# A state-space layer with routed experts: one written order of single operations for TensorE, VectorE and ACT, and expert blocks behind the eighth round

## The chip, the core and the metric

The kernel runs on one core of a Trainium2 chip. A core has five engines with queues of their own: TensorE (PE) for matrix products, with a separate row in the profile for its weight loads (PEld); VectorE (DVE); ScalarE (ACT); GpSimd (POOL); and SyncE (SP), which issues DMAs. An engine works through its own queue in order and waits on semaphores for the others. Products land in PSUM, which this kernel uses as eight tiles (banks) of 512 float32 columns; everything else lives in SBUF. The metric is the device time of one execution in microseconds, and the figure for a kernel is the median of several executions.

## What is computed

4096 tokens of 256 features go through a Mamba-style layer, a layer norm, a mixture of eight experts of which each token takes one, and a second layer norm. Cut to what matters:

```python
xz = x @ W_in                                   # 256 -> 1024: conv half, gate half
conv = silu(causal_conv4(xz[:, :512]) + conv_b)
d = conv @ W_x                                  # 33 columns: delta, B (16), C (16)
delta = softplus(d[:, :1])
h_t = exp(delta * -exp(A_log)) * h_(t-1) + delta * B * conv[:, :16]
ssm = sum(h_t * C, over the 16 states)
y = (ssm + conv * D_param) * silu(xz[:, 512:])
x1 = layernorm(x + y @ W_out)
e = argmax(x1 @ Wr.T + br)                      # one of eight experts
out = layernorm(x1 + relu(x1 @ W1[e].T + b1[e]) @ W2[e].T + b2[e])
```

## The kernel before

The tokens are cut into eight blocks of 512 (`TB`, `NB`), and each block passes through stages in successive rounds of the loop over `k` (line 1047). In round `k` block `k` is projected, block `k-1` (called `a`) gets its state scan, block `k-2` (`b`) its gate and output projection, and block `k-3` (`c`) its place in the experts' lists. The pieces are functions:

- `project(i, c)` (line 729): chunk `c` of eight of the input projection, into one of three PSUM banks with the tag `mm`. For chunks 0 to 3 ACT then copies it to `xc` (line 761) and starts the convolution in `acc` (763); DVE adds three taps (`taps`, 720) and ACT applies Silu (772). For chunks 4 to 7 ACT applies Silu for the gate (759).
- `gauge` (780) projects to delta, B and C; `gauge_out` (794) turns the result by TensorE transposes, and a run of small DVE operations works out softplus by a series (lines 815 to 837), each on 128 x 4 numbers and mostly on the one before it. ACT gives the exponential (816).
- `scan` (841): transposes (846), the decay's exponential on ACT (848), the scan on DVE (852), and the product with C as two pieces `hC` of 256 columns (860).
- `gate` (865): two pairs of float32 products with a matrix of ones, 16 rows each (872), sum over the states; DVE adds the skip (879), and DVE or POOL multiplies with the gate (884).
- `look` and `look_out` (886, 901) work out the router's share of x; `router_behind` (484) works out W_out times the router's weights in two halves of small products, in rounds 1 and 2.
- `project_out(i, j)` (916): output projection of 128 tokens, residual, statistics; with the last of four, the layer norm's rows and their store to DRAM. `choose` (948) picks the expert, `rank` (974) and `place` (1014) enter each token in its expert's list. The row masks of line 1008 run on POOL, and on DVE for the last three blocks.
- `table` (284), called by `blocks_of` (1027), turns counts into a table of expert blocks of 128 rows; `tokens_of` (1036) looks up the rows. 17 of the 32 blocks can be known before the last tokens are placed (`EARLY`).
- `blocks` (680) runs the expert blocks in quarters: `expert(n)` (714) advances by n. Weights are fetched by POOL's indirect DMAs (522) into three slots, rows by line 504; results are scattered by line 650.

The order on TensorE is the one written here, by the `manual_schedule` of line 120. The orders on DVE, ACT and POOL come from the scheduler, which takes what it thinks is ready first. The expert quarters of the first blocks stand between the projections of rounds 6 and 7:

```python
fill = {NB - 2: (0, 0, 0, 0, 0, 0, 2, 2), NB - 1: (1, 1, 2, 1, 1, 1, 1, 1)}.get(k, (0,) * 8)
```

Behind the loop the last blocks' stages drain between further quarters, written out one by one (lines 1112 to 1156).

These banks are three with the tag `mm`, three with `o` (state sums, output projections, expert outputs) and two with `tr` (everything small or turned).

Of the kernel before, what the change touches and what calls it, by code (L numbers as in the profile page):

```python
# [37 lines left out]
F32 = mybir.dt.float32  # L38
# [9 lines left out]
P = 128  # L48
# [45 lines left out]


# [4 lines left out]
def mamba_moe(  # L100
# [142 lines left out]
    nc.gpsimd.memset(sr, 0.0)  # L243
    ones8 = const.tile([P, NE], F32, name="ones8")
# [239 lines left out]
    def router_behind(half):  # L484
        po = bank("tr", f"pwo{half}", 2)
        pov = po[:, 0 : CC * NE].rearrange("p (c e) -> p c e", e=NE)
        cs = slice(half * CC // 2, (half + 1) * CC // 2)
        for c in range(CC)[cs]:
            for dc in range(DC):
                nc.tensor.matmul(  # L490
                    pov[:, c, :], lhsT=woutT[:, dc, c * P : (c + 1) * P], rhs=wr[:, dc, 0:NE],
                    start=(dc == 0), stop=(dc == DC - 1),
                )
        nc.scalar.copy(wout[:, cs, D : D + NE], pov[:, cs, :])

# [224 lines left out]
    def taps(i, c):  # L720
        acc, xc = st[i]["acc", c], st[i]["xc"]
        for k in range(KC - 1):
            nc.vector.scalar_tensor_tensor(  # L723
                acc, xc[:, c, k : k + TB], cw[:, c, k : k + 1], acc, ALU.mult, ALU.add
            )

    banks = {}

    def project(i, c):
# [3 lines left out]
        if c == 0:  # L733
            if i == 0:
                s["xc"] = a2.tile([P, CC, KC - 1 + TB], F32, tag="xc", name="xc0")
                nc.gpsimd.memset(s["xc"][:, :, 0 : KC - 1], 0.0)
            s["cv"] = a3.tile([P, CC, TB], F32, tag="cv", name=f"cv{i}")
            s["sg"] = a3.tile([P, CC, TB], F32, tag="sg", name=f"sg{i}")
        xc, cv, sg = s["xc"], s["cv"], s["sg"]
# [17 lines left out]
        pm = banks.pop(c)  # L757
        if c >= CC:
            evicted = nc.scalar.activation(sg[:, c - CC, :], pm, AF.Silu)  # L759
        else:  # L760
            nc.scalar.copy(xc[:, c, KC - 1 :], pm)  # L761
            acc = a3.tile([P, TB], F32, tag="acc", name=f"acc{i}_{c}")
            evicted = nc.scalar.activation(  # L763
                acc, pm, AF.Identity, scale=cw[:, c, KC - 1 : KC], bias=cb[:, c : c + 1]
            )
            s["acc", c] = acc
            if c < CC - 1:
                taps(i, c)
        if ("acc", c - 2) in s:

            with tc.issue_after(evicted.ins):
                nc.scalar.activation(cv[:, c - 2, :], s["acc", c - 2], AF.Silu)
        if c == CC and i + 1 < NB:

            after = st[i + 1]["xc"] = a2.tile(
                [P, CC, KC - 1 + TB], F32, tag="xc", name=f"xc{i + 1}"
            )
            nc.gpsimd.tensor_copy(after[:, :, 0 : KC - 1], xc[:, :, TB : TB + KC - 1])

    def gauge(i):  # L780


        s_, cv = st[i], st[i]["cv"]
        px = bank("tr", f"px{i}", 2)
        for c in range(CC):
            g = c % 2 * H
            nc.tensor.matmul(
                px[g : g + H, :], lhsT=wx[:, c, :], rhs=cv[:, c, :],
                start=(c < 2), stop=(c >= CC - 2), tile_position=(0, g),
            )  # L790
        s_["pxs"] = a2.tile([P, TB], F32, tag="pxs", name=f"pxs{i}", bufs=1)
        nc.scalar.copy(s_["pxs"], px)

    def gauge_out(i):

        s_ = st[i]
        px = bank("tr", f"pxo{i}", 2)
        for j in range(JT):
            at = slice(j * P, (j + 1) * P)
            nc.tensor.transpose(px[:, at], s_["pxs"][:, at], ident)  # L800
        pxv = px.rearrange("p (j h n) -> p j h n", h=P // H, n=H)

        def by_state(a):
            return a.unsqueeze(2).to_broadcast([P, JT, NS])

        xd = a2.tile([P, JT, XW], F32, tag="xd", name=f"xd{i}", bufs=1)

        parts = a2.tile([P, JT, 2, XW], F32, tag="parts", name=f"parts{i}", bufs=1)
        nc.scalar.copy(parts, pxv[:, :, :, 0:XW])
        nc.vector.tensor_tensor(xd, parts[:, :, 0, :], parts[:, :, 1, :], ALU.add)  # L810
        nc.scalar.copy(sr[:, :, RC : RC + NS], xd[:, :, 1 + NS : XW])
        x0 = xd[:, :, 0]

        e = a2.tile([P, JT], F32, tag="e", name=f"e{i}")
        nc.vector.scalar_tensor_tensor(e, x0, -1.0, x0, ALU.mult, ALU.min)
        grown = nc.scalar.activation(e, e, AF.Exp)
        if i == 0:
            with tc.issue_after(grown.ins):
                nc.scalar.activation(nega, al, AF.Exp)
            nc.vector.tensor_scalar(nega, nega, -1.0, None, ALU.mult)  # L820
        s = a2.tile([P, JT], F32, tag="s", name=f"s{i}")
        nc.vector.tensor_scalar(s, e, 2.0, None, ALU.add)
        nc.vector.reciprocal(s, s)
        nc.vector.tensor_tensor(s, s, e, ALU.mult)
        w = a2.tile([P, JT], F32, tag="w", name=f"w{i}")
        nc.vector.tensor_tensor(w, s, s, ALU.mult)
        q = a2.tile([P, JT], F32, tag="q", name=f"q{i}")
        nc.vector.tensor_scalar(q, w, LOG_SERIES[-1], None, ALU.mult)
        for a in LOG_SERIES[-2::-1]:
            nc.vector.scalar_tensor_tensor(q, q, a, w, ALU.add, ALU.mult)  # L830
        nc.vector.scalar_tensor_tensor(q, q, 1.0, s, ALU.add, ALU.mult)
        delta = a2.tile([P, JT], F32, tag="delta", name=f"delta{i}")
        nc.vector.tensor_scalar(delta, x0, 0.0, None, ALU.max)
        nc.vector.scalar_tensor_tensor(
            sr[:, :, RD : RD + NS], by_state(q), 2.0, by_state(delta), ALU.mult, ALU.add
        )
        nc.vector.tensor_tensor(
            sr[:, :, RB : RB + NS], xd[:, :, 1 : 1 + NS], sr[:, :, RD : RD + NS], ALU.mult
        )

    def scan(i):
        s_, cv = st[i], st[i]["cv"]
        hbefore = st[i - 1]["h"] if i else None
        pt = bank("tr", f"pt{i}", 2)
        for j in range(JT):
            nc.tensor.transpose(pt[0:NR, j * P : (j + 1) * P], sr[:, j, :], ident)
        dA = a2.tile([NS, TB], F32, tag="dA", name=f"dA{i}", bufs=1)
        nc.scalar.activation(dA, pt[RD : RD + NS, :], AF.Exp, scale=nega)
        dBx = a2.tile([NS, TB], F32, tag="dBx", name=f"dBx{i}", bufs=1)
        nc.vector.tensor_tensor(dBx, pt[RB : RB + NS, :], cv[0:NS, 0, :], ALU.mult)  # L850
        h = a2.tile([NS, TB], F32, tag="h", name=f"h{i}")
        nc.vector.tensor_tensor_scan(
            h, dA, dBx, 0.0 if hbefore is None else hbefore[:, TB - 1 : TB],
# [353 lines left out]
```

## Time and profile before

| | |
|---|---|
| median of three executions | 479.17 us (476.85 to 479.68) |
| the profiled execution | 479.7 us, its span 478.0 us |
| mean granted TensorE clock | 0.993 |
| first projection product | 4.4 us |
| last projection product | 225.3 us |
| ACT table loads of line 759 (Silu) | 12, mean 1283 ns |
| DVE taps, line 723 | 96, mean 777 ns |
| POOL row masks, line 1008 | 20, mean 1307 ns |
| TensorE's waits for DVE's `sg` ahead of line 920 | 0.9 us, once |

The span runs from the first to the last instruction; the execution's own time has 1.7 us around it. A row of the profile's groups names the source line, the engine, the operation, then output and inputs by the program's names; behind the bar stand busy time and the mean of one. TensorE's matmul rows overlap, so the time that one of them holds the engine is read from the starts of neighbours in the timeline. A float32 product is recorded as two rows.

### The profile page before, as it was taken

The numbers are of one execution on the slowest core, as the hardware profiler recorded it, in microseconds if no ns is written. First come the engines' busy times: TensorE is split into PE (matmuls) and PEld (weight loads), VectorE is DVE, ScalarE is ACT, GpSimd is POOL, SyncE is SP. The second block draws the span as 40 slices with busy tenths as digits, with TensorE's granted clock in tenths as the row PEclk, the third lists the DMA queues.
The fourth block names the chain that finished last, engine by engine and source line by source line (L and its number), as shares of the span: only waits on it lengthen the run. The fifth ranks groups of instructions, "written<-read, shape, count | busy, mean of one in ns | idle before, by whom it ended". The sixth has DMA issues, their size and how long they took to land. (4 is left out here: it accounts for less than half of the span.)

```text
span 478.0 us, 7559 instructions
## 1 busy us (share of the span) xinstructions
PE 466.2 (98%) x2606; PEld 350.1 (73%) x2606; DVE 340.4 (71%) x1120; ACT 223.4 (47%) x453; POOL 185.5 (39%) x194
## 2 busy tenths in 40 slices
PE   8999999999999999999999999999999999999994
PEld 6444554645455566677788999999989898989884
DVE  1687959899898997986998978755446565645453
ACT  3776767886896877584625131212212121212111
POOL 2001203442418372450433423435445456654541
PEclk9998999999999999999999999999999999999998
DMA  8401012040124945250766759799997279977910
GB/s 237 166 1 45 0 42 91 1 132 0 47 87 149 431 159 188 110 199 18 271 242 225 270 209 366 260 368 350 359 347 277 60 253 345 313 247 245 353 44 22
DMA packets 23401, 89.98 MB, mean 188 GB/s; under 512 B 4914, under 2 KB 14909, under 8 KB 19650
## 3 DMA queue, kind: packets, MB, share of 16 engines
q0 software_dynamic: 8752, 74.71, 42.7%
q1 hardware_dynamic: 13650, 14.50, 9.3%
q8 instruction: 21, 0.34, 0.3%
q10 hardware_dynamic: 960, 0.27, 0.3%
q14 instruction: 18, 0.15, 0.1%
HBM read 87.78 MB, written 9.43 MB: 203 GB/s over the span
## 5 line engine op out<-in xcount | busy, mean ns | idle before, releaser
L744 PE MATMUL pm<-xTb,win 128*128 128x512 f32 (+1 forms) x264 | 122.5, 598 | 0.0
L587 PEld LDWEIGHTS ph<-xgT,we 128*128 128x128 f32 x864 | 100.8, 192 | 5.5 <-DVE r L637 1.3
L587 PE MATMUL ph<-xgT,we 128*128 128x128 f32 x864 | 103.0, 276 | 0.0
L612 PE MATMUL pe<-we,hT 128*128 128x256 f32 x432 | 98.9, 380 | 0.0
L612 PEld LDWEIGHTS pe<-we,hT 128*128 128x128 f32 x432 | 79.7, 190 | 10.0 <-DVE lg L960 0.3
L723 DVE SCALAR_TENSOR_TENSOR acc<-xc,cw,acc 128x512 f32<-128x512 f32 x96 | 72.6, 777 | 15.7 <-DMA wx<-in_W_x 8.6
L744 PEld LDWEIGHTS pm<-xTb,win 128*128 128x128 f32 x264 | 49.2, 195 | 45.5 <-issue 40.8
L262 ACT ACTIVATE sdm<-mvm,eps 128x1 f32<-128x1 f32 x32 | 9.4, 294 | 122.6 <-DVE mvm L260 116.8
L522 POOL DMA_INDIRECT we<-in_experts,widx x32 | 33.6, 1049 | 85.0 <-DVE r L637 24.9
L920 PE MATMUL po<-wout,sg 128*128 128x264 f32 x256 | 64.1, 392 | 1.0 <-DVE sg L884 0.9
L884 POOL TENSOR_TENSOR sg<-cv,sg 128x512 f32<-128x512 f32 x22 | 32.7, 1492 | 59.6 <-DVE cv L879 46.1
L920 PEld LDWEIGHTS po<-wout,sg 128*128 128x128 f32 x256 | 46.1, 190 | 11.0 <-issue 2.9
L650 POOL DMA_INDIRECT out<-y,tidx x32 | 32.9, 1027 | 38.5 <-DVE y L264 30.5
L598 DVE TENSOR_SCALAR hT<-ph,we 128x128 f32<-128x128 f32 x108 | 31.3, 341 | 20.7 <-PE ph L587 20.6
L637 DVE TENSOR_TENSOR r<-pe,xs 128x256 f32<-128x256 f32 x32 | 13.5, 422 | 43.9 <-PE pe L612 43.8
L504 POOL DMA_INDIRECT xg<-x1d,tidx x32 | 31.9, 998 | 29.7 <-DVE xd L810 7.5
L596 ACT ACTIVATE hT<-ph,we 128x128 f32<-128x128 f32 x108 | 30.8, 368 | 23.2 <-PE ph L587 20.7
L1008 POOL TENSOR_SCALAR rowh<-lrow,row,code 128x256 f16<-128x256 bf16 x20 | 26.0, 1307 | 27.9 <-DVE row L1000 26.7
L879 DVE SCALAR_TENSOR_TENSOR cv<-cv,dp,py 128x256 f32<-128x256 f32 x64 | 28.5, 469 | 3.4 <-PE py L872 3.4
L759 ACT ACTIVATE sg<-pm 128x512 f32<-128x512 f32 x32 | 19.1, 596 | 19.5 <-PE pm L744 17.0
L761 ACT COPY xc<-pm 128x512 f32<-128x512 f32 x32 | 18.6, 582 | 19.1 <-PE pm L744 18.8
L763 ACT ACTIVATE acc<-pm,cb,cw 128x512 f32<-128x512 f32 x32 | 25.1, 784 | 0.0
(219 smaller groups left out, 604.4 us busy)
## 6 DMA issues: line engine op xcount, KB each, us to landing
xb<-in_x SPq DMA_DIRECT2D x8, 512.0 KB, 6.1
x1d<-x SPq DMA_DIRECT2D x8, 512.0 KB, 4.8
xTb<-in_xT SPq DMA_DIRECT2D x7, 512.0 KB, 3.3
win<-in_W_in SPq DMA_DIRECT2D x1, 512.0 KB, 5.2
we<-in_W_outT SPq DMA_DIRECT2D x1, 512.0 KB, 5.9
wout<-in_W_out SPq DMA_DIRECT2D x1, 512.0 KB, 6.9
we<-in_experts,widx POOLq DMA_INDIRECT x32, 10.3
xg<-x1d,tidx POOLq DMA_INDIRECT x32, 6.6
```

Source lines behind the costliest of these rows:

```text
L504: nc.gpsimd.indirect_dma_start(out=to, out_offset=None, in_=x1d[0:rows, :], in_offset=bass.IndirectOffsetOnAxis(ap=at, axis=0),)
L522: nc.gpsimd.indirect_dma_start(out=wes[n][:, :], out_offset=None, in_=experts, in_offset=bass.IndirectOffsetOnAxis(ap=weights[n], axis=0), ...
L587: nc.tensor.matmul(ph[:, n * w : (n + 1) * w], lhsT=we[:, at : at + P], rhs=xgT[:, dc * w : (dc + 1) * w], start=(dc == 0), stop=(dc == DC ...
L596: nc.scalar.activation(hT[:, fc, :], ph[:, n * w : (n + 1) * w], AF.Relu, bias=bias)
L598: last[b] = nc.vector.tensor_scalar(hT[:, fc, :], ph[:, n * w : (n + 1) * w], bias, 0.0, ALU.add, ALU.max)
L612: nc.tensor.matmul(py[:, 0:D], lhsT=hT[:, fc, 0:P], rhs=out_weights(fc), start=(fc == 0), stop=(fc == FC - 1),)
L650: moved = nc.gpsimd.indirect_dma_start(out=out, out_offset=bass.IndirectOffsetOnAxis(ap=at, axis=0), in_=rows, in_offset=None, bounds_chec ...
L723: nc.vector.scalar_tensor_tensor(acc, xc[:, c, k : k + TB], cw[:, c, k : k + 1], acc, ALU.mult, ALU.add)
L744: nc.tensor.matmul(banks[c][:, at], lhsT=win[:, dc, c * P : (c + 1) * P], rhs=xTb[:, dc, at], start=(dc == 0), stop=(dc == DC - 1),)
L879: nc.vector.scalar_tensor_tensor(cv[:, c, at], cv[:, c, at], dp[:, c : c + 1], py[:, 0 : TB // 2], ALU.mult, ALU.add,)
L884: eng.tensor_tensor(sg[:, c, :], cv[:, c, :], sg[:, c, :], ALU.mult)
L920: nc.tensor.matmul(po[:, 0 : D + NE], lhsT=sg[:, c, j * P : (j + 1) * P], rhs=wout[:, c, :], start=(c == 0), stop=(c == CC - 1),)
```

## The change

A round is now one list, `ROUND`, of 125 entries, each with the name of a step, its arguments and, behind the colon, how many blocks it lags. The functions above are taken apart so that one step issues one operation, or the products of one group. In rounds 1 to 7 DVE and ACT keep the written order as TensorE does; POOL and SP are not in it. From round 8 the eight places of `project` issue one expert quarter each, and twelve rounds are run. A block's stages spread over five rounds: gate and output projection at a lag of 2, layer norm, choice and ranks at 3, place at 4.

The products with C become one piece of 512 columns in rows 0 to 15 of a zeroed tile `parts_`. Two subtractions put what is left behind the upper 16 bits into rows 32 to 47 and 64 to 79, and one bf16 product with ones over all 128 rows, reading only the upper halves, sums the states. The skip works on 512 columns. `router_behind` goes; `look` is used for W_out too, in round 1. The row masks are all on DVE, and the gate's chunk 3 alone is on DVE. The rows of x are loaded a round later.

```diff
+ROUND = """
+    project.0:0 look_copy:1 root:3 columns_hot:4 tap.3.0:1 inverse_root:3 rows_hot.0:4
+    gated.1:2 look_turn:2 project.1:0 begin.0:0 tap.3.1:1 place:4 logits:3 look_parts:2
+    tap.3.2:1 biased:3 project.2:0 conv.3:1 skip.3:2 best_logit:3 enter:4 keep.0:0 is_best:3
+    skip.0:2 order_best:3 keep.2:0 gauge:1 gated.3:2 begin.2:0 tap.0.0:0 project.3:0
+    begin.1:0 first_best:3 shift_rows:3 one_hot:3 look_sum:2 count:3 skip.2:2 count_on:3
+    gauge_copy:1 gauge_turn:1 tap.2.0:0 tap.0.1:0 keep.1:0 gated.0:2 gauge_parts:1
+    gauge_sum:1 keep.3:0 tap.1.0:0 minus_abs:1 gated.2:2 project.4:0 project_out.1:2
+    tap.2.1:0 exp_abs:1 put_c:1 add_two:1 positive:1 invert:1 tap.0.2:0 conv.0:0
+    keep_rows.0:3 ratio:1 rank:3 silu.0:0 own_rank:3 square:1 project_out.0:2 tap.2.2:0
+    keep_rows.2:3 series.0:1 rank_sum:3 add_rows.1:2 series.1:1 add_rows.0:2 series.2:1
+    whole_rank:3 series.3:1 project_out.2:2 stats.1:2 series.4:1 keep_rows.1:3 column_of:3
+    project.5:0 tap.1.1:0 series_end:1 row_of:3 gather_stats.1:2 put_delta:1 rows_hot.2:3
+    put_b:1 tap.1.2:0 state_turn:1 keep_rows.3:3 load_rows:1 decay:1 rows_hot.1:3 drive:1
+    begin.3:0 stats.0:2 project_out.3:2 states:1 conv.1:0 rows_hot.3:3 weighted:1
+    add_rows.2:2 gather_stats.0:2 conv.2:0 project.6:0 look:0 silu.2:0 project.7:0 rest.1:1
+    add_rows.3:2 rest.2:1 halo:0 state_sum:1 stats.3:2 stats.2:2 gather_stats.3:2 skip.1:1
+    gather_stats.2:2 silu.1:0 silu.3:0
+"""
+COUNTED = 3
...
+    def weighted(i):
+        nc.vector.tensor_tensor(
+            parts_[0:NS, :], st[i]["pt"][RC : RC + NS, :], st[i]["h"], ALU.mult
+        )
+
+    def upper(rows):
+
+        return parts_[rows, :].bitcast(BF16).rearrange("p (t two) -> p t two", two=2)[:, :, 1]
+
+    def rest(i, n):
+        at = slice((n - 1) * Q, (n - 1) * Q + NS)
+        nc.vector.tensor_tensor(
+            parts_[n * Q : n * Q + NS, :], parts_[at, :], upper(at), ALU.subtract
+        )
+
+    def state_sum(i):
+        py = st[i]["py"] = bank("o", f"py{i}")
+        nc.tensor.matmul(py, lhsT=oneb, rhs=upper(slice(0, P)), start=True, stop=True)
+
+    def skip(i, c):
+        cv = st[i]["cv"]
+        nc.vector.scalar_tensor_tensor(
+            cv[:, c, :], cv[:, c, :], dp[:, c : c + 1], st[i]["py"], ALU.mult, ALU.add
+        )
+
+    def gated(i, c):
         cv, sg = st[i]["cv"], st[i]["sg"]
...
+        eng = nc.vector if c in (3,) else nc.gpsimd
+        eng.tensor_tensor(sg[:, c, :], cv[:, c, :], sg[:, c, :], ALU.mult)
...
+    def one_round(r):
+
+        for entry in ROUND.split():
+            name, behind = entry.split(":")
+            i = r - int(behind)
+            name, *at = name.split(".")
+            at = [int(n) for n in at]
+            if not 0 <= i < NB:
+                if name == "project" and i >= NB:
+                    expert()
+                continue
+            if i == 0 and name in ("look", "look_copy"):
+                continue
+            steps[name](i, *at)
+            if name == "project":
+                if r == 0 and at[0] == 2:
+                    router_weights()
+                if r == 0 and at[0] == 5:
+                    look(0)
+                    look_copy(0)
+                if r == 1 and at[0] == 3:
+                    look("w")
+                    look_copy("w")
+                if r == 1 and at[0] == 6:
+                    look_turn("w")
+                    look_parts("w")
+                    look_sum("w")
+                if r == NB - 1 and at[0] == 4:
+
+                    turn(0)
+
+    def in_order():
+        return tc.manual_schedule(engines={mybir.EngineType.DVE, mybir.EngineType.Activation})
+
+    LAST = 12
+    for r in range(LAST):
+        with ExitStack() as order_:
+            if 0 < r < NB:
+                order_.enter_context(in_order())
+            if have(r + 1):
+                load(r + 1)
+            if r == 0:
+                load_later()
+            one_round(r)
+        if have(r - COUNTED):
+            blocks_of(r - COUNTED)
     expert(2)
...
+    tokens_of(NB - 1)
```

The other steps issue the operations of the functions before, with the same operands: `keep`, `begin`, `tap`, `conv` and `silu` those of `project` and `taps`; `gauge` to `put_b` those of `gauge` and `gauge_out`; `state_turn` to `states` those of `scan`; `add_rows` to `keep_rows` those of `project_out`; `logits` to `count_on` those of `choose`; `own_rank` to `rows_hot` those of `rank`. `enter` adds to the lists and calls `tokens_of` for its block.

## What I expect, and why

> **What bounds the kernel now.** I read the page's busy table and clock row first, then windows cut at the first projection matmul of each round, then TensorE's timeline inside the rounds.
>
> ```profile
> span 478.0 us, 7559 instructions
> PE 466.2 (98%) x2606; PEld 350.1 (73%) x2606; DVE 340.4 (71%) x1120; ACT 223.4 (47%) x453; POOL 185.5 (39%) x194
> ...
> PEclk9998999999999999999999999999999999999998
> ...
> 20.80:40.20 19.40, 18.73 (x67) 8.41 (x66) 11.35 (x29) 15.37 (x29) 0.47 (x1) 1.00 0.08 28
> 40.20:69.00 28.80, 28.61 (x104) 15.50 (x103) 22.27 (x54) 18.49 (x31) 4.99 (x4) 0.94 0.05 19
> 69.00:95.70 26.70, 26.70 (x109) 14.58 (x107) 24.26 (x71) 22.03 (x37) 9.37 (x8) 1.00 0.18 60
> 95.70:123.20 27.50, 26.55 (x110) 14.26 (x108) 24.98 (x72) 21.65 (x36) 10.52 (x8) 1.00 0.18 57
> 123.20:150.30 27.10, 26.67 (x112) 14.40 (x110) 25.55 (x92) 21.69 (x36) 11.87 (x10) 1.00 0.19 60
> 150.30:185.40 35.10, 34.47 (x168) 21.88 (x166) 31.44 (x96) 27.05 (x48) 18.22 (x15) 1.00 0.68 259
> 185.40:225.70 40.30, 40.30 (x201) 27.53 (x200) 32.43 (x101) 24.79 (x43) 14.65 (x12) 1.00 0.38 140
> 225.70:471.50 245.80, 244.81 (x1690) 221.90 (x1688) 157.47 (x588) 60.43 (x181) 110.69 (x111) 1.00 0.73 264
> ...
> 44.80:48.20 3.40, 3.40 (x7) 0.77 (x7) 3.40 (x6) 0.81 (x2) 2.34 (x2) 0.50 0.01 2
> ```
>
> In the windows the columns are length, then busy time of PE, weight load, DVE, ACT, POOL, the granted clock, DMA share and GB/s. TensorE is busy nearly everywhere, so only its work and its gaps count; but its busy time hides short gaps (matmuls overlap), so I use starts. The last two parts of the page matter little: after 225.7 us only drain and expert blocks run, at a full clock.
>
> ```profile
> 73.70 1.94 PE L787 MATMUL px<-cv,wx 128*64 128x512 f32 x8
> 75.57 3.70 PE L744 MATMUL pm<-xTb,win 128*128 128x512 f32 x8
> 79.11 0.60 PE L800 MATMUL pxo<-ident,pxs 128*128 128x128 f32 x4
> 79.54 1.95 PE L920 MATMUL po<-wout,sg 128*128 128x264 f32 x8
> 81.32 1.88 PE L744 MATMUL pm<-xTb,win 128*128 128x512 f32 x4
> ...
> 97.54 0.70 PE L872 MATMUL py<-hC,ones 16*128 16x256 f32 x4
> 98.17 1.99 PE L744 MATMUL pm<-xTb,win 128*128 128x512 f32 x4
> ```
>
> From start to start, a projection chunk is 1.72 (81.32 to 83.04 where the rank matmuls start), gauge 1.87, its turn 0.43, one output projection 1.78, the state sum 0.63 (97.54 to 98.17). In the same way look is 0.57, its turn 0.27, the state turn 0.44, place 0.44, rank 0.13. A full round is thus 8 x 1.72 + 1.87 + 0.43 + 4 x 1.78 + 0.63 + 0.57 + 0.27 + 0.44 + 0.44 + 0.13 = 25.7; with what is lost at changes of shape (0.1 behind gauge, 0.1 at each change of row count) I put it at 26.3, an estimate. The rounds took 26.7, 27.5 and 27.1: only 0.4 to 1.2 us each is stall. In the third window 3.4 us ran at half clock, which cost 1.7. An expert block is 7.24 us (two successive pe starts in the pure stage), a quarter 1.81.
>
> **The change, part by part.** Expert quarters cost TensorE 1.81 wherever they stand. Moving the 12 that ran in rounds 6 and 7 behind round 8 costs nothing by itself; what is lost is their use as filler. Round 6 without its 4 quarters and the lookup is 35.1 - 7.24 - 0.4 = 27.5; round 7 without 8, with its place behind the last projection, 40.3 + 0.4 - 14.5 = 26.2. Filler saved about 1 us, in round 7 alone.
>
> *bf16 state sum.* One bf16 matmul of 512 columns takes the place of 4 records. No row has it; bounds are 0.22 (half of an f32 record of 512 columns, 0.43, since f32 records come in pairs of two products) and 0.43. I take 0.22: 0.4 less in each of some 8 rounds. It adds two subtractions on DVE (16x512, by the dBx row 0.61 start to start, so 1.2 a round).
>
> *VectorE in order.* I added occupancies: a tap is 0.66 although its row says 0.74, because the next one starts before it ends; a small operation is 0.07 to 0.10.
>
> ```profile
> 77.29 0.74 DVE L723 SCALAR_TENSOR_TENSOR acc<-xc,cw,acc 128x512 f32<-128x512 f32 x1
> 77.95 0.18 DVE L965 TENSOR_TENSOR lg<-lg,back 128x32 f32<-128x32 f32 x1
> ```
>
> Taps 12 x 0.66 = 7.9; skip 4 x 0.66 = 2.6 (was 8 x 0.39); drive, scan and weighting 2.4; the subtractions 1.2; one gate product 0.6; residual adds and statistics 4 x (0.34 + 0.34 + 0.09) = 3.1; column mask 0.6; row masks 4 x 0.26 = 1.0 (they were 1.3 each on POOL); list sum 0.3; about 35 small ones 3.1. Sum 22.8 of a 25.9 us round. Before, DVE shows 24.3 to 25.6 of 27, since a small operation that needs the one just ahead waits out its tail (0.2 instead of 0.07). In the new order no two neighbours depend on each other, so that cost goes.
>
> *ACT in order.* Its rows per round: 4 keeps 1.9, 4 begins 2.7, 8 Silu 4.0, 4 row copies 2.0, the rest 2.4, and 6 table loads. A load is 1.28, and the next starts at once:
>
> ```profile
> 222.79 1.28 ACT L934 ACT_TABLE_LOAD   x1
> 225.23 0.30 ACT L934 ACTIVATE sda<-mva,eps 128x4 f32<-128x4 f32 x1 [1.15 <-DVE mva L929]
> ```
>
> So ACT holds 13.0 + 6 x 1.29 = 20.7. The Trainium skill (ScalarE: Activation LUTs, "What ACT_TABLE_LOAD costs") speaks against this: about 2.66 us for each switch, load plus drain. By that ACT would hold 29.0, more than TensorE's round, every round would be 3 us longer and the sum +16 instead of -2.5. The trace shows no such drain, so I take 1.29. The rows show too that the load (222.79) runs while its user still waits for an operand of DVE (until 225.2); exp in gauge and in decay then costs its chain 0.2 and 0.7 only.
>
> *A steady round laid out.* With TensorE's steps end to end (project.0 at 0, gauge 5.8, gauge_turn 9.8, project_out.1 12, state_turn 19.2, project.6 21.3, state_sum 25.5) I put the two lists beside it, with 0.1 for a hop (the gauge's last product gave way at 26.23, its copy started at 26.37). Gauge_parts ends at 10.7, exp at 12.6, the series at 17.9, put_b at 18.5: 0.6 before state_turn. Decay ends at 20.5, the scan at 21.9, the second subtraction at 24.8: 0.6 before state_sum. The last gate product on POOL ends near 9.9, 2 before project_out.1 needs it; begin.3, queued on ACT behind decay, ends at 21.2, hardly before project.6 may need that bank. DVE loses 2.9 to waits inside and stays in step. So the layout fits with slacks of 0.1 to 2; I charge 0.2 a round for the thin ones.
>
> *Rounds 2 to 7.* Full rounds go to 25.9: 27.5 to 25.9, 27.1 to 25.9, 27.5 to 26.0 (the lookup's copy stands in ACT's order), 26.2 to 25.9. Round 3 has no place yet: 26.7 to 25.5. Round 2 loses its four-chunk router product and two waits: 27.0 without the clock's share to 25.4. Sum -7.4, +1.2 for thin slacks, = -6.2.
>
> *Round 1* pays. There are no output projections yet, so TensorE has only project.4 and .5 between gauge_turn and state_turn. Before, the same chain took
>
> ```profile
> 29.76 0.60 PE L800 MATMUL pxo<-ident,pxs 128*128 128x128 f32 x4
> ...
> 38.07 0.61 PE L846 MATMUL pt<-ident,sr 128*80 128x128 f32 x4 [0.67 <-ACT rx L899]
> ```
>
> 8.3 us from start to start, mostly covered by two projections more, the router product and look. Now look_copy of W_out stands before begin.1 and gauge_copy on ACT and needs project.3 and look (9.8); gauge_turn slips to 11.5, a stall of 1.7. The chain behind it, some 6.6 with the taps between, ends at 18.5, while TensorE is ready at 15.4: 3.1 more. The round comes to 18.7 work + 4.9 = 23.6, against 19.4: +4.2. Bounds: 0 if that work were ready early (nothing in the order allows it), +6 with the before's whole 8.3.
>
> *Tables and drain.* Two state sums less in the drain with one moved up: -1.0. A block table's 17 small operations fall between two ordered rounds: +0.5. DMA: weights (2.2 MB a block) now flow only in the pure stage, whose 7.24 us blocks were already fed at up to 350 GB/s without a gap; nothing. On POOL the 20 row masks (26.0 in all) go away; chunk 1's gate product of blocks 6 and 7 comes to it (1.5 each), between weight and row gathers of 1.0 each, with 2 to spare before TensorE needs it: nothing, or about 1 a time if a gather that waits for a block's end stands ahead. Row loads of x go out a round later on SP behind the x1d store, and are needed a round later still; nothing, or 6 us once if not.
>
> Sum: -6.2 + 4.2 - 1.0 + 0.5 = -2.5. The profiled execution took 479.7, its span of 478.0 and 1.7 around it, and stands 0.5 above the median of 479.17; I set the sum against the median: 476.7.
>
> **Rivals.** *Clean start* (0.28): round 1 loses little because DVE reaches the series earlier, and the thin slacks hold: -7.4 + 1.5 - 1.0 = -6.9, with 0.8 from the drain, 471.5. For it: in the early windows DVE is half idle. Against: the wait for look is written into ACT's list. *ACT's order becomes a wait in every round* (0.20): begin.3 behind decay. If state_turn or the load comes 1.3 late, project.6 waits for chunk 3's bank and the scan for decay. It decides from 0.5 us a round (-2.5 + 6 x 0.5 above zero), costs 1% from 1.2 (+4.7), and at 1.9 gives 488. For it: slack there is 0.1. Against: the rows of loads that run ahead. *Round-1 gap halves the clock again* (part of the range): The Trainium skill (TensorE: Matmul & The Clock Gate, "What's actually happening") lets the clock fall after an idle window of about 3.4 us. The trace had one half-clock stretch of that length with TensorE thinly used before it; by the rule the 3.1 us gap could give one more, 1.7, by the trace one as before, which I take. *Not what it says* (0.10): the order isn't held or the tables' operations break it up, and rounds stay near 27 with round 1's loss: 478 to 482.
>
> **How the numbers follow.** About 1% is what a measurement tells from no change: under 474.4 or over 484.0. My sum has 0.42 (473 to 480). Faster: the clean start's 0.28 and a quarter of my own case, 0.39. Slower: ACT's wait and a little of the last, 0.22. Rest 0.39. The range, 467 to 488, leaves out the ends of both outer cases.
>
> **What would show it.** Windows of rounds 3 to 7 near 26 with equal lengths; a gap of about 3 us ahead of the state turn in round 1; DVE neighbours 0.07 apart in the series; ACT row begin behind decay with no TensorE wait behind it. It is wrong if rounds are 27 or more, if the state turn or state sum waits over 1 us in each round, or if the drain differs by over 2.

## The result, and the profile after

| | before | after |
|---|---|---|
| median of four executions | 478.97 us (476.85 to 479.68) | 502.17 us (501.91 to 503.77) |
| span of the profiled execution | 478.0 us | 502.0 us |
| mean granted TensorE clock | 0.993 | 0.980 |
| last projection product | 225.3 us | 211.6 us |
| last TensorE instruction | 471.3 us | 495.4 us |

The ratio is 1.0499, interval 1.0459 to 1.0539: slower by 23 us, where 2.5 us less was predicted. The page of the changed kernel, first its busy times and the clock's row:

```profile
PE 468.0 (93%) x2576; PEld 348.9 (69%) x2576; DVE 351.5 (70%) x1115; ACT 217.8 (43%) x450; POOL 166.7 (33%) x177
...
PEclk9998999999999999988979999999999999999998
```

TensorE's share falls from 98% to 93%, and the clock's row has a dip in its middle that before did not have. Windows cut at each round's first projection, rounds 1, 3, 5, 6 and 7 and then the first part of the drain:

```profile
19.90:46.80 26.90, 20.73 (x68) 8.39 (x67) 14.38 (x34) 17.58 (x31) 0.44 (x1) 0.94 0.06 20
...
72.80:99.30 26.50, 25.33 (x97) 13.69 (x97) 24.94 (x70) 21.93 (x36) 5.42 (x4) 1.00 0.19 61
...
126.80:154.30 27.50, 26.09 (x107) 14.07 (x106) 26.34 (x73) 21.69 (x36) 5.92 (x4) 1.00 0.19 61
154.30:186.10 31.80, 27.44 (x111) 14.45 (x110) 29.55 (x95) 21.62 (x37) 13.46 (x11) 1.00 0.69 271
186.10:212.10 26.00, 25.91 (x106) 14.05 (x105) 25.20 (x72) 20.00 (x33) 5.31 (x3) 1.00 0.13 41
212.10:260.50 48.40, 39.35 (x232) 32.19 (x231) 43.04 (x158) 17.44 (x40) 14.28 (x12) 0.89 0.35 126
```

The full rounds are not at 25.9 but at 27.5; DVE (fourth column) is busy for 26.3 of it. Round 1 is 26.9 instead of 19.4. In the first 48 us of the drain TensorE is idle for 9, at a clock of 0.89.

Taking the 12 moved quarters (21.7 us) out of before's rounds, the span's +24.0 splits so: rounds 0 and 1 +6.6, rounds 2 to 7 +1.5 (before 163.8, after 165.3), from the last round to the last TensorE instruction +16.0 (267.3 to 283.3).

**Where a steady round waits.** The timeline of round 5, VectorE and GpSimd (start, duration, engine, what; idle time in brackets):

```profile
128.02 0.72 DVE L780 SCALAR_TENSOR_TENSOR acc<-xc,cw,acc 128x512 f32<-128x512 f32 x1
128.09 1.77 POOL L943 TENSOR_TENSOR sg<-cv,sg 128x512 f32<-128x512 f32 x1 [16.13 <-DVE cv L936]
...
128.74 1.20 DVE L1119 TENSOR_SCALAR rowh<-lrow,row,code 128x256 f16<-128x256 bf16 x1
129.87 0.74 DVE L780 SCALAR_TENSOR_TENSOR acc<-xc,cw,acc 128x512 f32<-128x512 f32 x1
...
133.41 1.75 POOL L943 TENSOR_TENSOR sg<-cv,sg 128x512 f32<-128x512 f32 x1 [3.55 <-DVE cv L936]
133.96 1.76 DVE L780 SCALAR_TENSOR_TENSOR acc<-xc,cw,acc 128x512 f32<-128x512 f32 x1
```

The row mask of 128.74 takes 1.20 us where the next one takes 0.34, and the tap of 133.96 takes 1.76 where its neighbours take 0.74. Each begins while a gate product of POOL runs, and ends behind it: the mask at 129.94, the product at 129.86; the tap at 135.72, the product at 135.16. The record of the DVE operation is long: this shows as busy time, not as a wait. About 3 us of such a round goes so. The end of the same round, TensorE, VectorE and ACT:

```profile
146.01 0.61 PE L892 MATMUL pt<-ident,sr 128*80 128x128 f32 x4
146.35 1.28 ACT L899 ACT_TABLE_LOAD   x1
...
147.65 0.68 ACT L899 ACTIVATE dA<-pt,nega 16x512 f32<-16x512 f32 x1
...
148.24 1.88 PE L743 MATMUL pm<-xTb,win 128*128 128x512 f32 x4
148.36 0.68 DVE L904 TENSOR_TENSOR dBx<-pt,cv 16x512 f32<-16x512 f32 x1 [0.97 <-ACT dA L899]
...
152.10 0.68 DVE L926 TENSOR_TENSOR parts__144<-parts__144 16x512 f32<-16x512 f32 x1
...
152.81 0.43 DVE L999 TENSOR_TENSOR xb<-po,xb 128x264 f32<-128x264 f32 x1
...
153.27 0.68 DVE L926 TENSOR_TENSOR parts__144<-parts__144 16x512 f32<-16x512 f32 x1
...
154.01 0.39 PE L932 MATMUL py<-parts__144,oneb 128*128 128x512 bf16 x1 [1.41 <-DVE parts__144 L926]
```

The exponential's table is loaded only when the state turn is nearly done, the drive on DVE starts when the decay on ACT has ended, a residual add stands between the two subtractions, and the state sum waits 1.41 us. By TensorE's starts each of the sums that end rounds 2 to 7 loses 1.0 to 1.6.

**Where the drain waits.** TensorE's timeline of rounds 8 and 9, then windows at the same places:

```profile
222.99 1.00 PE L469 MATMUL pi<-pick,lists 128*128 128x8 f32 x4 [2.70 <-DVE best L1052]
...
257.88 0.99 PE L469 MATMUL pi<-pick,lists 128*128 128x4 f32 x4 [3.60 <-DVE lg L1055]
```

```profile
219.60:223.00 3.40, 0.70 (x5) 0.30 (x3) 3.40 (x23) 0.29 (x1) 0.00 (x0) 1.00 0.00 0
223.00:229.80 6.80, 6.80 (x17) 3.51 (x18) 5.56 (x14) 2.30 (x6) 3.52 (x3) 0.50 0.07 19
...
257.10:263.90 6.80, 6.02 (x20) 5.33 (x21) 4.14 (x19) 2.47 (x6) 1.66 (x2) 0.50 0.18 62
```

`pi` is the lookup in `tokens_of`. Around the first wait DVE is busy for all of 3.40 us with 23 operations, most of them small. The clock is at half for 6.8 us behind the first wait, and for 6.8 us from 0.8 before the end of the second, which costs about 3.4 and 3.0 more. By starts these two places make 6.6 of waiting and 6.4 of clock, most of the drain's +16.0; the rest is in the state sums (1.41 at 213.6 us and 1.14 at 247.6) and in 0.99 at 301.9, less about 1 that before waits in its own drain.

The second wait is not for want of TensorE work alone. Ahead of it stands this on DVE and POOL:

```profile
251.41 3.11 DVE L402 TENSOR_TENSOR starts<-ends,whole 128x8 f32<-128x8 f32 x1
...
251.99 2.49 POOL L943 TENSOR_TENSOR sg<-cv,sg 128x512 f32<-128x512 f32 x2
```

An operation of the block table on 128 x 8 numbers, which takes 0.15 at its shortest, took 3.11 and ended with two gate products of POOL (254.5). The lookup needs the table.

### The profile page after: what moved, and what is told of

The parts are those of the page before. It is cut to its first block, busy times and chain, and to the rows that moved or that the text cites. A ratio compares the mean times of both kernels' runs of the same rounds, so it can differ in the third digit from the quotient of the medians.

```text
span 502.0 us, 7489 instructions
## 1 busy us (share of the span) xinstructions
PE 468.0 (93%) x2576; PEld 348.9 (69%) x2576; DVE 351.5 (70%) x1115; ACT 217.8 (43%) x450; POOL 166.7 (33%) x177
## 4 chain that ended last, share of the span: by engine, by line
PE 55%; DVE 32%; ACT 7%; issue 4%; DMA 1%; POOL 0%; POOLq 0%; SPq 0%; ACTq 0%
PE ph L599 21%; PE pe L624 19%; DVE acc L780 9%; PE pm L743 6%; PE po L992 3%; DVE cv L936 2%; DVE parts__144 L926 2%; ACT x L1026 2%; DVE h L911 2%; DVE sta L1005 2%; PE px L805 1%; DVE xb L999 1%; PE pf L635 1%; ACT L899 1%; DVE rowh L1119 1%
## 5 line engine op out<-in xcount | busy, mean ns | idle before, releaser
L624 PE MATMUL pe<-we,hT 128*128 128x256 f32 x432 | 101.2, 388 | 0.0
L780 DVE SCALAR_TENSOR_TENSOR acc<-xc,cw,acc 128x512 f32<-128x512 f32 x96 | 81.1, 857 | 17.5 <-ACT xc L762 12.8
L624 PEld LDWEIGHTS pe<-we,hT 128*128 128x128 f32 x432 | 81.7, 195 | 12.1 <-issue 1.6
L743 PEld LDWEIGHTS pm<-xTb,win 128*128 128x128 f32 x264 | 47.6, 192 | 52.7 <-issue 36.4
L943 POOL TENSOR_TENSOR sg<-cv,sg 128x512 f32<-128x512 f32 x24 | 37.4, 1564 | 140.2 <-DVE cv L936 123.0
L992 PE MATMUL po<-wout,sg 128*128 128x264 f32 x256 | 61.5, 389 | 0.3 <-POOL sg L943 0.2
L610 DVE TENSOR_SCALAR hT<-ph,we 128x128 f32<-128x128 f32 x108 | 31.1, 343 | 25.8 <-PE ph L599 24.2
L516 POOL DMA_INDIRECT xg<-x1d,tidx x32 | 33.1, 1035 | 36.2 <-DVE xs L642 15.1
L608 ACT ACTIVATE hT<-ph,we 128x128 f32<-128x128 f32 x108 | 30.9, 368 | 21.7 <-PE ph L599 13.3
L790 ACT ACT_TABLE_LOAD x21 | 26.9, 1283 | 7.1 <-DVE s L852 6.8
L936 DVE SCALAR_TENSOR_TENSOR cv<-cv,dp,py 128x512 f32<-128x512 f32 x32 | 23.3, 735 | 0.5 <-PE py L932 0.5
L599 PE MATMUL ph<-wide,we 128*128 128x136 f32 (+1 forms) x160 | 21.6, 293 | 0.5 <-DVE r L649 0.5
L599 PEld LDWEIGHTS ph<-wide,we 128*128 128x128 f32 x160 | 21.2, 190 | 1.1 <-DVE r L649 0.9
```

Of the source, the lines that this page charges most:

```text
L516: nc.gpsimd.indirect_dma_start(out=to, out_offset=None, in_=x1d[0:rows, :], in_offset=bass.IndirectOffsetOnAxis(ap=at, axis=0),)
L599: nc.tensor.matmul(ph[:, n * w : (n + 1) * w], lhsT=we[:, at : at + P], rhs=xgT[:, dc * w : (dc + 1) * w], start=(dc == 0), stop=(dc == DC ...
L608: nc.scalar.activation(hT[:, fc, :], ph[:, n * w : (n + 1) * w], AF.Relu, bias=bias)
L610: last[b] = nc.vector.tensor_scalar(hT[:, fc, :], ph[:, n * w : (n + 1) * w], bias, 0.0, ALU.add, ALU.max)
L624: nc.tensor.matmul(py[:, 0:D], lhsT=hT[:, fc, 0:P], rhs=out_weights(fc), start=(fc == 0), stop=(fc == FC - 1),)
L743: nc.tensor.matmul(banks[c][:, at], lhsT=win[:, dc, c * P : (c + 1) * P], rhs=xTb[:, dc, at], start=(dc == 0), stop=(dc == DC - 1),)
```

## The experiments

The times of before differ between chips (478.8, 484.0 and 483.6 us), so each ratio stands against runs of before on its own chip. "E1" below means the first edit, kept as a base.

**All gate products on VectorE**

```diff
-        eng = nc.vector if c in (3,) else nc.gpsimd
+        eng = nc.vector
```

> All four gate products on VectorE, none on GpSimd; nothing else changed. Theory A (a VectorE operation that starts beside a GpSimd gate product stands still until that one ends, three times a round, about 1.0 us each, and this lateness reaches the state sum): VectorE pays 3 x 0.6 us a round and loses about 3.0, taps are back at a mean of 740 to 780 ns from 857, TensorE's wait ahead of the state sum falls from 1.4 us to under 0.7 in rounds 4 to 7, and the table's operations in round 8 are early; 502 goes to 486 to 494. Theory B (the chain decay, drive, scan, weighting, two subtractions is too long by itself): the wait stays at 1.2 to 1.7 us, 499 to 504.

Measured: 493.68 us, ratio 1.0318 (1.0284 to 1.0352), 8.5 us under after (before took 478.78 there and 478.97 beside after), though DVE does 24 operations more. Groups of VectorE and TensorE in this kernel, and below it of after (line, engine, what, shapes and count, then busy time and mean):

```profile
L780 DVE SCALAR_TENSOR_TENSOR acc<-xc,cw,acc 128x512 f32<-128x512 f32 x96 | 70.1, 743 | 15.9 <-ACT xc L762 13.3 <-ACT acc L774 2.5
L943 DVE TENSOR_TENSOR sg<-cv,sg 128x512 f32<-128x512 f32 x32 | 21.8, 682 | 0.0
...
L932 PE MATMUL py<-parts__144,oneb 128*128 128x512 bf16 x8 | 3.1, 387 | 3.8 <-DVE parts__144 L926 3.8
```

```profile
L780 DVE SCALAR_TENSOR_TENSOR acc<-xc,cw,acc 128x512 f32<-128x512 f32 x96 | 81.1, 857 | 17.5 <-ACT xc L762 12.8 <-ACT acc L774 3.4 <-POOL sg L943 1.2
L943 POOL TENSOR_TENSOR sg<-cv,sg 128x512 f32<-128x512 f32 x24 | 37.4, 1564 | 140.2 <-DVE cv L936 123.0 <-DVE up L326 17.1
...
L932 PE MATMUL py<-parts__144,oneb 128*128 128x512 bf16 x8 | 3.1, 389 | 9.0 <-DVE parts__144 L926 9.0
```

The taps' mean falls from 857 to 743 ns, the long records are gone, and the state sums wait 3.8 instead of 9.0 in all. So 24 products moved to DVE cost it less than leaving them to POOL. Rounds 3 to 5 fall from 26.5, 27.5 and 27.5 to 25.8, 26.3 and 26.3.

The profiled span is 10.6 shorter: 5.2 in rounds 2 to 7 and 6.6 in the drain, less 1.3 that rounds 0 and 1 took more. In the drain the table operation of 3.11 takes 0.16 again, the wait of 3.60 behind it is 0.60, and one half-clock stretch of 3.4 us is left of the two of 6.8. Of the drain's +16.0, 9.4 stay.

**The same in the kernel before**: `eng = nc.vector` at its line 883.

> The kernel before with all its gate products on VectorE. Theory A in the other kernel: VectorE stands still 13.5 us in all beside GpSimd there too, in 24 instructions, and it pays 22 x 0.6 = 13.2 us for the products; TensorE seldom waits for it, so 477 to 482, same. If the lock costs the kernel before as it costs the changed one (8.5 us): 470 to 474.

Measured: 483.94 us, ratio 0.9994 (0.9958 to 1.003). Its taps fall from 777 to 744 ns as well, and its time doesn't move. Before has fewer long records to win back: DVE's busy time goes from 340.4 to 337.8 with 22 products more (after to E1: 351.5 to 344.1 with 24 more), and in its rounds TensorE's longest wait for either engine is 0.95 us. So moving the products is worth something in the new order and nothing in the old; what the long records alone cost in before, this run can't tell.

**A float32 state sum without subtractions**

```diff
-    add_rows.2:2 gather_stats.0:2 conv.2:0 project.6:0 look:0 silu.2:0 project.7:0 rest.1:1
-    add_rows.3:2 rest.2:1 halo:0 state_sum:1 ...
+    add_rows.2:2 gather_stats.0:2 conv.2:0 project.6:0 look:0 silu.2:0 project.7:0
+    add_rows.3:2 halo:0 state_sum:1 ...
...
-        nc.tensor.matmul(py, lhsT=oneb, rhs=upper(slice(0, P)), start=True, stop=True)
+        nc.tensor.matmul(py, lhsT=ones[0:NS, :], rhs=parts_[0:NS, :], start=True, stop=True)
```

> The two subtractions are out, and the state sum is one float32 product over 16 rows (0.86 us on TensorE in place of 0.22). Theory B: the wait ahead of the state sum goes to under 0.2 us in every round, rounds 4 and 5 fall from 27.5 to 26.4 to 26.8; 502 goes to 492 to 497. Theory A: VectorE is still held up by GpSimd; the wait shrinks but 0.5 us or more of it stays there or shows ahead of the state turn, 497 to 501.

Measured: 501.74 us, ratio 1.047 (1.0417 to 1.0523), as after. The state sum no longer waits, and rounds 2 to 7 are 3.4 us shorter in all, although the float32 sum holds TensorE for 1.07 by starts where the bf16 sum holds it for 0.23 (154.01 to 154.24). But rounds 0 and 1 are 2.4 longer, for a reason that stays open, and the drain takes as long as in after, with waits of 3.5 and 3.9 ahead of `pi`. Without the subtractions the wait goes, but the dearer product takes part of it back (0.6 a round is left of a wait of 1.0 to 1.6), and the total time shows nothing of it.

**The lookup behind the round's last step**

```diff
     def enter(i):
         nc.vector.tensor_tensor(lists, lists, st[i]["pz"][:, 0 : LH * P], ALU.add)
-        if i < NB - 1:
-            tokens_of(i)
...
             one_round(r)
+        if have(r - 4) and r - 4 < NB - 1:
+            tokens_of(r - 4)
         if have(r - COUNTED):
             blocks_of(r - COUNTED)
```

> The row lookups of the expert blocks stand behind the round's last step and not behind the list sum early in the round. Theory C (the lookups meet a table that VectorE has not finished; TensorE stands 2.7 and 3.6 us in rounds 8 and 9, and each time two clock windows of 3.4 us run at half speed): these two waits and both half-clock stretches go, round 6 loses about 2 us; 502 goes to 486 to 491. Rival (VectorE is late for everything in these rounds, so that another wait takes their place): the half clock stays, 497 to 502.

Measured: 497.99 us, ratio 1.04 (1.0365 to 1.0435), 4.2 us under after. The waits ahead of `pi` are gone, but others stand in the drain instead:

```profile
221.51 1.94 PE L805 MATMUL px<-cv,wx 128*64 128x512 f32 x8 [2.19 <-DVE xgT L579]
236.38 0.60 PE L892 MATMUL pt<-ident,sr 128*80 128x128 f32 x4 [1.44 <-DVE sr L883]
243.36 0.39 PE L932 MATMUL py<-parts__144,oneb 128*128 128x512 bf16 x1 [0.92 <-DVE parts__144 L926]
254.82 1.16 PE L992 MATMUL po<-wout,sg 128*128 128x264 f32 x4 [0.91 <-POOL sg L943]
257.82 2.01 PE L992 MATMUL po<-wout,sg 128*128 128x264 f32 x4 [1.84 <-POOL sg L943]
```

Gauge, state turn, state sum and output projections now wait for DVE or POOL, and one half-clock stretch of 3.4 us is left of the two of 6.8. So the place of the lookup is worth 4.2, in part by the clock, and is not the whole cause: the waits move to other stages, two of them to gate products that POOL has not finished.

**No written order on VectorE and ACT**: the two lines that enter `in_order` removed.

> VectorE and ACT are left to the scheduler in every round, as before; the steps, the stages, the bf16 sum and the place of the expert blocks stay. Theory D (the written order is what costs): 478 to 488. Theory A, B and C (the gate products beside VectorE, the long state chain and the lookups cost, whoever orders): 495 or more; I expect 494 to 508.

Measured: 506.85 us, ratio 1.0595 (1.0551 to 1.0639), 4.7 us over after. In rounds 3 to 5 the state turn then waits 1.6 to 1.8 us and the state sum 0.9, and rounds 2 to 7 are 4.8 longer in all. Rounds 0 and 1, of which only the second had a written order, are 2.1 longer, and the drain is 3.4 shorter. The written order helps in the full rounds; it is not what makes the changed kernel slow.

**E1, with two quarters at each place of the drain**

```diff
                 if name == "project" and i >= NB:
-                    expert()
+                    expert(2)
```

> Gate products on VectorE as in the first experiment, and from round 8 each place of a projection issues two expert quarters and not one. Theory E (the drain stands because too little expert work lies between the steps of the last blocks' chains; before, 12 quarters were spent in rounds 6 and 7 and the drain had two at its first places): TensorE's waits of 2.3, 1.7, 0.9, 0.8 and 0.6 us behind round 7 and the half-clock stretch go; 493.7 goes to 484 to 488. Rival (VectorE's queue is full in the drain, and two quarters bring it as much work as TensorE): the waits move to other rows, 492 to 496.

Measured: 501.41 us, ratio 1.0363 (1.0303 to 1.0423). Both halves of the answer are in TensorE's timeline:

```profile
207.65 0.39 PE L932 MATMUL py<-parts__144,oneb 128*128 128x512 bf16 x1 [0.42 <-DVE parts__144 L926]
255.99 1.13 PE L624 MATMUL pe<-we,hT 128*128 128x256 f32 x4 [0.43 <-DVE hT L610]
```

```profile
351.24 0.53 PE L469 MATMUL pi<-pick,lists 128*128 128x27 f32 x4
358.86 0.45 PE L567 MATMUL pg<-ident,xg 128*128 128x128 f32 x1 [7.09 <-DMA xg<-x1d,tidx]
```

In E1 rounds 8 and 9 had waits of 2.29 and 0.60 ahead of `pi`, 1.70 ahead of the state turn and 0.92 ahead of the state sum; here 0.43 is the longest up to 320 us. But with two quarters at all 32 places, 66 of the 68 that don't need the last lookup are used when it comes. The next block's rows are gathered only behind it, TensorE waits 7.1 us for that DMA, another 4.4 at 370 us, and the clock is at half for 10.2 us (5 of them within the wait) and for 3.4.

**E1, with W_out's look later in round 1**

```diff
-                if r == 1 and at[0] == 3:
+                if r == 1 and at[0] == 5:
                     look("w")
                     look_copy("w")
-                if r == 1 and at[0] == 6:
+                if r == 1 and at[0] == 7:
                     look_turn("w")
```

> Gate products on VectorE, and in round 1 the router's look at W_out stands behind project.5 and not behind project.3, so that gauge_copy needn't wait for it on ACT. The prediction's reading of round 1: the 1.65 us wait ahead of the gauge's turn goes, look fills 0.6 us of the wait ahead of the state turn; round 1 falls from 27.7 to 25.3 to 26, 493.7 goes to 490.5 to 492.5. Rival (the whole of it returns ahead of the state turn, where the chain on VectorE ends): round 1 stays at 27 or more.

Measured: 495.11 us, ratio 1.0253 (1.0165 to 1.0341). E1's 1.0318 lies inside this interval, so no difference can be told in time. In the profile round 1 is 25.3 instead of E1's 27.7, but E1 had a half-clock stretch of 6.8 us there and this kernel one of 3.4; the run with two quarters has E1's round 1 with 3.4, and takes 26.3. So the edit is worth about 1.0: the wait at the gauge's turn is gone, 2.97 ahead of the state turn stays, and 2.19 ahead of the state sum is new.

**E1, with round 1 out of the written order**: `if 1 < r < NB:`.

> Gate products on VectorE, and round 1 left to the scheduler on VectorE and ACT (rounds 2 to 7 stay written). If the written order makes round 1 slow: 27.7 goes to 22 or less, 493.7 to 488 or less. If it is the place of the state turn, two projections behind the gauge's turn where it had three and a router product before: 24 to 26, with a wait of 2.5 to 3.5 us ahead of the state turn left; 490.5 to 493.

Measured: 498.42 us, ratio 1.0326 (1.0266 to 1.0385), as E1. Round 1 falls to 24.2, but round 0 rises to 18.0, and the state turn still waits 3.3. DVE's and ACT's order doesn't make that wait. That leaves the state turn's place on TensorE, which the last run but one moves.

**"Look later", with two quarters in rounds 8 and 9 only**: E1 and W_out's look as above, and

```diff
-                    expert()
+                    expert(2 if r < NB + 2 else 1)
```

> All gate products on VectorE, W_out's look moved as before in f2, and the drain's rounds 8 and 9 issue two expert quarters at each of the eight places, rounds 10 and 11 one. Theory (the drain's one quarter of 1.81 us is too little to cover each stage's chain on VectorE; two are enough; the last lookup needs quarters left over): the waits ahead of pi, pt, py and po in the drain (8.3 us together in f2) go, and as 50 quarters instead of 66 are used before the last lookup, the 7.3 and 4.4 us waits of g1 at 351 and 370 us don't come: f2's ratio of 1.025 less 7/484 gives 1.011. Rival (the waits are a debt of the chain itself and move to the next place where quarters are few, as with the late lookup): they come back in rounds 10 and 11 or at the last lookup, ratio 1.02 or more.

Measured: 488.95 us, ratio 1.0108 (1.006 to 1.0157), as the theory had it: 7 us under "look later" by the ratios, each against before on its own chip (by the two profiles the drain is 4.6 shorter). The same places in TensorE's timeline:

```profile
218.61 0.51 PE L469 MATMUL pi<-pick,lists 128*128 128x8 f32 x4
237.88 0.60 PE L892 MATMUL pt<-ident,sr 128*80 128x128 f32 x4
247.35 0.39 PE L932 MATMUL py<-parts__144,oneb 128*128 128x512 bf16 x1
...
259.92 0.51 PE L469 MATMUL pi<-pick,lists 128*128 128x4 f32 x4
```

No brackets: none of them waits, and the waits of 7.1 and 4.4 don't come, since 18 quarters are left at the last lookup.

**In round 1, projection 6 ahead of the state turn**, on top of that:

```diff
-        for entry in ROUND.split():
+        entries = ROUND.split()
+        if r == 1:
+            for name in ("begin.3:0", "project.6:0"):
+                entries.remove(name)
+                entries.insert(entries.index("state_turn:1"), name)
+        for entry in entries:
```

> As h3, and in round 1 alone begin.3 and the projection of chunk 6 stand ahead of the state turn, so three projections instead of two lie between the gauge's turn and it. Theory (round 1 pays for the place of the state turn): the wait of 3.0 us ahead of pt in round 1 falls to 1.0 to 1.3, round 1 from 25.3 to 23.6, ratio 0.004 under h3. Rival (the wait is VectorE's own chain, and what stands behind the turn only moves): the state sum of round 1 then waits 2 us more, round 1 stays at 25 and the ratio is h3's.

Measured: 489.22 us, ratio 1.0095 (1.0054 to 1.0137); against the run before, no difference can be told in time. In the profile round 1 falls from 25.3 to 23.5 and the state turn waits no more:

```profile
34.67 1.98 PE L743 MATMUL pm<-xTb,win 128*128 128x512 f32 x4 [1.13 <-ACT sg L793]
...
36.49 0.60 PE L892 MATMUL pt<-ident,sr 128*80 128x128 f32 x4
```

Part of the wait moved: 1.13 ahead of projection 6, until ACT's Silu of a gate chunk ends, and by starts 1.2 ahead of W_out's turn; the state sum's 2.19 stays, and the half-clock stretch of 3.4 us now lies at 42.7 to 46.1 us, for the most part in round 2, which is 1.3 longer. Rounds 1 and 2 together are 0.5 shorter. Both the theory and its rival held in part.

**The two subtractions next to each other**, on top of that: `rest.1:1 rest.2:1` written in a row, the residual add behind them.

> As h4, and the two subtractions stand next to each other, the residual add of 0.43 us behind them instead of between. Theory (what is left of the state sum's wait, 0.42 to 0.58 us a round, is that add in VectorE's order): the waits of rounds 2 to 7 fall by 0.4 each, 2.5 us in all, ratio 0.005 under h4. Rival (the second subtraction waits for the first one's result anyway, and the late decay sets the end): the second starts 0.3 us earlier at most, the waits fall by 0.2 or less and the ratio moves by less than 0.002.

Measured: 489.44 us, ratio 1.0119 (1.006 to 1.0177); again no difference in time can be told. Both answers missed: the state sum's wait rose. First this kernel, then the one before it, VectorE and TensorE at the end of round 4:

```profile
121.64 0.68 DVE L927 TENSOR_TENSOR parts__144<-parts__144 16x512 f32<-16x512 f32 x1
122.35 0.75 DVE L781 SCALAR_TENSOR_TENSOR acc<-xc,cw,acc 128x512 f32<-128x512 f32 x1
123.14 0.68 DVE L927 TENSOR_TENSOR parts__144<-parts__144 16x512 f32<-16x512 f32 x1
...
123.87 0.39 PE L933 MATMUL py<-parts__144,oneb 128*128 128x512 bf16 x1 [0.74 <-DVE parts__144 L927]
```

```profile
120.75 0.68 DVE L926 TENSOR_TENSOR parts__144<-parts__144 16x512 f32<-16x512 f32 x1
121.47 0.43 DVE L999 TENSOR_TENSOR xb<-po,xb 128x264 f32<-128x264 f32 x1
121.93 0.68 DVE L926 TENSOR_TENSOR parts__144<-parts__144 16x512 f32<-16x512 f32 x1
...
122.67 0.39 PE L932 MATMUL py<-parts__144,oneb 128*128 128x512 bf16 x1 [0.42 <-DVE parts__144 L926]
```

The subtractions are not neighbours in the trace: a tap now stands in the gap, in place of the residual add. It is 0.32 longer than the add, and the wait is 0.32 longer (0.74 against 0.42). That agrees with the theory by its number, with the opposite sign, and shows that the written order isn't kept to the letter on DVE. A kernel with nothing between the subtractions was not run.

No version beats before; the nearest is at 1.0095. What is left there can be read beside the profile of before with its gates on DVE, from another chip whose before takes 484.0 against 483.6. From the last round to the last TensorE instruction both take 274.6 us, with quarters counted alike (h4: 204.3 to 478.9; before: 222.7 less 21.7 to 475.6). The spans differ by 3.3 us: round 1 (+4.1), round 6 with its tables and lookup (29.8 against 34.7 less 7.2, +2.3) and -2.8 in rounds 3 to 5, the rest in rounds 0, 2 and 7. By the medians the difference is nearer to 5; the profiled execution of this kernel was one of its faster ones (487.34).

## Why the prediction was wrong

The range of 467 to 488 did not hold the time. Two steps failed: the steady round, in which POOL's gate products cost DVE nothing, and the drain, in which one expert quarter at each place was too little between the stages. In the prediction's own sum, rounds 2 to 7 were to give -6.2, round 1 +4.2 and tables and drain -0.5; measured are +1.5, +6.6 (with round 0) and +16.0. With the gates on DVE they are -3.7, +7.9 and +9.4. Point by point:

- **What bounds it, and TensorE's work: right.** Round 7, where little waits, took 26.0, and with the gates on DVE the full rounds are 25.8 to 26.3, against the predicted 25.9. The bf16 product holds TensorE for 0.23, predicted 0.22.
- **"A steady round laid out": failed.** It gave 0.6 of slack ahead of the state sum; the trace has 1.0 to 1.6 of wait. The term that failed most is the gate on POOL. I checked when its result would be ready, and costed it at nothing; but POOL held DVE for about 3 us of each round, so DVE's 22.8 became 26.3. The Trainium skill (GPSIMD Engine Reference, "8. Key points") names the shared SBUF interfaces of VectorE and GpSimd, with contention for DVE instructions in a 2-port performance mode or with two SBUF inputs. The taps read two inputs in SBUF, and the trace agrees for them (0.74 became 1.76). The row to ask was in before's trace too, where the taps' mean of 777 ns stood above the single 740. E1 shows its price here: 8.5 us in the whole kernel by the medians, more than half of it in the drain.
- **The drive on DVE waits for the decay on ACT.** Before's groups already had that wait, 3.1 us in eight times; the layout ran the two side by side. After has 7.9 in eight. Each subtraction also holds DVE for 0.71 (152.10 to 152.81), not the 0.61 that I took. With E1 the state sum's wait still was 0.58 by starts, for these reasons and the operation between the subtractions. The prediction saw no two dependent neighbours in the new order; in the trace the operations that keep them apart are themselves on the chain.
- **ACT: right in its duration.** It is busy for 21.7 of a full round, predicted 20.7, and a table load is 1.28. The 29.0 that the skill's figure would give was rightly turned down. That loads run while their users wait held only in part: the load of 146.35 starts behind a layer-norm row that ACT does first, when the state turn is nearly over, and the decay comes with it.
- **Round 1: mechanism right, size off.** 4.9 of loss was predicted, at the gauge's turn and the state turn; these two waits are 1.65 and 3.38. The rest of the 8.2 lost is 1.0 at W_out's turn, 0.45 at the state sum and 1.7 by a half-clock stretch, which the prediction had put into the range, not the sum. The state turn's place behind only two projections makes its wait: with one more ahead of it the wait is gone, but 2.2 of it comes back at other places, and no time is gained that can be told.
- **Moving the 12 quarters "costs nothing by itself; what is lost is their use as filler": mis-sized.** Filler was put at about 1 us. The prediction priced the filler at the place that they leave, round 7, and not at the place that the stages of blocks 6 and 7 then drain in. In the drain of after only one quarter of 1.81 stands between two stages. Of the +16.0 there 6.6 is POOL's; of the other 9.4, E1's waits of 2.29, 1.70, 0.92, 0.78 and 0.60 make 6.3 and its half-clock stretch 1.7. Two quarters removed those waits (1.0253 to 1.0108, the two on chips of their own), and in the best version the drain is as long as in before with its gates on DVE. The +0.5 for tables was mis-sized also: round 6 is still 2.3 longer when everything else is mended.
- **The rivals.** ACT's order with begin.3 behind the decay does not show: projection 6 starts at 148.24 with no wait, as begin.3 starts (148.23 to 148.99), so it does not need the bank that begin.3 still reads, as that rival took it to. No rival was about DVE slowed by POOL or about the drain: tables and drain stood at -0.5 in sum, with at most about 1 a time for POOL's gathers and 6 once for a late row load above it. The range ended 14 us short. The signs of being wrong that it named all came: rounds of 27.5, a state sum that waits over 1 us, a drain that differs by more than 2.

## What to carry to other kernels

Work that can be moved has a worth of its own as filler: before moving it, list the waits that it stands beside, and price the place it leaves and the place it goes to, with the clock lost behind each gap. An operation given to GpSimd was not off VectorE's path here; look for VectorE records longer than their own minimum (1.76 against 0.71 us for a tap, 3.11 against 0.15 for an operation of the table), in the drain as well as in the rounds. In a written order the slack of a chain has to be measured against records of the same chain, its waits among them, not against the sum of its durations.

## What the hardware showed unexpectedly

- VectorE operations that started beside a GpSimd product of 1.75 us didn't slow down in proportion; they ended behind it: 0.34 became 1.20, 0.74 became 1.76, and in the drain 0.15 became 3.11 (begun beside an indirect DMA issue of GpSimd, ended with the two products behind it). The tap that was already running (128.02, 0.72) wasn't lengthened, nor was a reciprocal of 128 x 4 numbers that started beside the product (128.66, 0.17).
- Half-clock stretches came as 3.4, 6.8 and 10.2 us, most of them behind or within TensorE waits of 1.8 to 7.1 us; the wait of 2.7 cost 3.4 more by it. They don't come with each such wait: at the same place in round 8, 2.29 in E1 was followed by 3.4 us of half clock and 2.30 in "look later" by none. And before's own stretch (44.8 to 48.2 us) had no wait ahead of it; TensorE was busy for 3.2 of the 3.4 us before.
- On the two chips of the later runs TensorE waits 2.3 to 2.6 us ahead of an expert product between 418 and 431 us, in four kernels with the new order and in before with its gates on DVE. In the profiles of before, after and E1, from other chips, it doesn't, and in two more from one of the later chips (two quarters at each place, and round 1 out of the order) it doesn't either. The cause is open.
